# Gates of the last stage in three groups of 12, 9 and 4 tiles, and three tiles more closed by TensorE

## The chip, the cores and the metric

The kernel runs on one core of a Trainium2 chip. A core has engines that run side by side and wait for each other through semaphores: TensorE (PE, matrix products; PEld is its weight load), VectorE (DVE), ScalarE (ACT), GpSimd (POOL) and SyncE (SP), which here only issues DMAs. Each engine takes its instructions in the order in which they stand in its queue. The metric is the device time of one execution in microseconds (us); lower is better.

## The reference

A two-layer graph network over 3125 nodes with 256 features and 50000 edges. Each layer adds to x a graph convolution, an attention over all nodes and a feed-forward part. The change lies in the last of these, the feed-forward part of layer 1, which is a mixture of four experts:

```python
def _forward(x, edge_index, W_gat, att_src, att_dst, b_gat, ln_gamma, ln_beta, W1, b1, W2, b2):
    ...
    agg = segment_sum(msg, dst, num_segments=M).reshape(M, HEADS * NUM_EXPERTS) + b_gat
    scores = _layernorm(agg, ln_gamma, ln_beta).reshape(M, HEADS, NUM_EXPERTS).mean(1)
    topk_s, topk_i = jax.lax.top_k(scores, TOP_K)
    w = jax.nn.softmax(topk_s, axis=-1)
    out = jnp.zeros_like(x)
    for ei in range(NUM_EXPERTS):
        g = jnp.where(topk_i == ei, w, 0.0).sum(-1)
        hh = jax.nn.gelu(x @ W1[ei] + b1[ei], approximate=False)
        out = out + g[..., None] * (hh @ W2[ei] + b2[ei])
    return out
```

`agg` comes from a small graph attention over edges that are sorted by their target node. The result of the whole network is x plus this `out`.

## The kernel before

The nodes lie in 25 tiles of 128 (the last holds 53), node on the partition. For DMAs the tiles form seven chunks, `CHUNKS`: tiles 0-3, 4-7, 8-11, 12-15, 16-18, 19-21 and 22-24, called chunks 0 to 6 here.

The last stage is `layer1_ffn`. All experts' outputs are computed for all nodes first (L1981 to L2022). The outputs of experts 0 and 1 stay in SBUF (`out0`, shown as `acc` in the profile, and `y1`, shown as `y`); those of experts 2 and 3 go to DRAM (`yd`) and are fetched back by chunks (`fetch`, L2227): chunks 0 to 2 into `yback`, chunks 3 to 5 into the memory of `xT`, chunk 6 into the `yback` that chunk 0 leaves. Beside the experts, POOL gathers and VectorE sums the attention's messages along the sorted edges. What is left then is the closing part, where the change is:

- L2291: for each of the 25 tiles POOL gathers the node's sums from DRAM, `g_r`, one gather after the other.
- `gates` (L2296) makes the four gates of the nodes of one group of tiles: some 36 small VectorE instructions over the whole group, and three steps on ACT: an exponential (L2308), a square root (L2329) and another exponential (L888). The root and the exponential behind it each need a table load on ACT. `gates` is a generator: it hands back control after the first exponential, after the root with the sums beside it, and after the ranks; whoever calls `next` decides what is put between.
- `by_rows` (L2362) closes one tile on VectorE: four instructions, each x += gate x expert output (L2366).
- `by_products` (L2370) closes tiles on TensorE: ACT scales the identity by a gate into a diagonal matrix, four for a tile (`diag`, L2381, three buffers); PE adds up x and the four diagonal products in PSUM (L2383, L2385), and ACT copies the sum back into x (L2373). The copy of a tile is put behind the diagonals of the next. It is a generator too, one tile for each `next`.
- `done` (L2352) counts the tiles of a chunk, and sends the chunk's rows of x to the output when the last has been closed (L2358, SP's queue). SP issues in the order in which `done` found the chunks complete in the program.

Four engines are scheduled by hand here: within PE, VectorE, ACT and SP the program's order is the queue's order, so where the `next` calls stand in lines L2392 to L2414 decides what waits behind what. Before the change the nodes have two groups, tiles 0 to 11 and 12 to 24. Products close tiles 0, 1, 2, 4, 5, 6, 8, 9, 10 of the first and 15, 17, 19, 21, 23 of the second; VectorE closes the eleven others by rows.

Of the kernel before, what the change touches and what calls it, by code (L numbers as in the profile page):

```python
# [23 lines left out]
NT = 25  # L24
# [111 lines left out]
class Kernel:  # L136
# [1795 lines left out]
    def layer1_ffn(self, acc=None):  # L1932
# [4 lines left out]
        with ExitStack() as c:  # L1937
# [358 lines left out]
            def gates(t0, n, out):  # L2296

                s = slice(t0, t0 + n)
                heads, each = [P, n, 4, 4], [P, n, 16]
                rs = r[:, s]  # L2300
                hasb = self.has[:, s, None].to_broadcast([P, n, 4])
                d = ga.tile([P, n, 4], F32, name=f"g_d{n}")
                nc.vector.tensor_sub(d, rs[:, :, 20:24], loop[:, s])
                c2 = ga.tile([P, n, 2, 4], F32, name=f"g_c2{n}")
                nc.vector.tensor_scalar(c2[:, :, 0, :], d, 0.0, None, op0=OP.min)
                nc.vector.scalar_tensor_tensor(c2[:, :, 1, :], d, 0.0, hasnt[:, s, None].to_broadcast([P, n, 4]),
                                               op0=OP.max, op1=OP.mult)
                nc.scalar.activation(c2, c2, AF.Exp)  # L2308
                yield
                nc.vector.tensor_mul(c2[:, :, 0, :], c2[:, :, 0, :], hasb)  # L2310
                nc.vector.tensor_mul(d, rs[:, :, 16:20], c2[:, :, 0, :])
                nc.vector.scalar_tensor_tensor(d, d, 1e-16, c2[:, :, 1, :], op0=OP.add, op1=OP.add)
                nc.vector.reciprocal(d, d)
                nc.vector.tensor_mul(c2, c2, d[:, :, None, :].to_broadcast([P, n, 2, 4]))
                agg = ga.tile(each, F32, name=f"agg{n}")
                own = ga.tile(each, F32, name=f"g_own{n}")
                for v, dest, i in ((rs[:, :, 0:16], agg, 0), (srow[:, s, 0:16], own, 1)):
                    nc.vector.tensor_mul(dest.rearrange("p t (h e) -> p t h e", h=4),
                                         v.rearrange("p t (h e) -> p t h e", h=4),
                                         c2[:, :, i, :, None].to_broadcast(heads))  # L2320
                nc.vector.tensor_add(agg, agg, own)
                nc.vector.tensor_add(agg, agg, vec["b_gat"][:, None, :].to_broadcast(each))
                mu = ga.tile([P, n], F32, name=f"s_mu{n}")
                nc.vector.tensor_reduce(mu, agg, AX.X, OP.add)
                nc.vector.scalar_tensor_tensor(agg, mu[:, :, None].to_broadcast(each), -1.0 / 16, agg,
                                               op0=OP.mult, op1=OP.add)
                nc.vector.tensor_mul(own, agg, agg)
                nc.vector.tensor_reduce(mu, own, AX.X, OP.add)
                nc.scalar.activation(mu, mu, AF.Sqrt, bias=self.eps, scale=1.0 / 16)  # L2329
                nc.vector.tensor_mul(agg, agg, vec["ln_gamma"][:, None, :].to_broadcast(each))  # L2330
                sc = ga.tile([P, n, NE], F32, name=f"s_sc{n}")
                nc.vector.tensor_reduce(sc, agg.rearrange("p t (h e) -> p t e h", h=4), AX.X, OP.add)
                yield
                nc.vector.reciprocal(mu, mu)
                nc.vector.tensor_mul(sc, sc, mu[:, :, None].to_broadcast([P, n, NE]))
                nc.vector.tensor_add(sc, sc, beta[:, None, :].to_broadcast([P, n, NE]))
                gate = self.softmax_parts(ga, sc, n, NE, f"s{n}")
                mask = self.top_two(ga, sc, n, NE, f"s{n}", tie)
                yield
                nc.vector.tensor_mul(gate, gate, mask)  # L2340
                self.normalise(ga, gate, n, NE, f"s{n}")
                out.append((gate, t0))
# [4 lines left out]
            def parts_of(t):  # L2347
                t0 = CHUNKS[chunk_of[t]][0]
                p, b = held(t), back[t0]
                return p, [out0[:p, t, :], y1[:p, t, :], b[:p, 0, t - t0, :], b[:p, 1, t - t0, :]]  # L2350

            def done(t):  # L2352
                i = chunk_of[t]
                left[i] -= 1
                if left[i] == 0:
                    t0, n = CHUNKS[i]
                    for s, p in pieces(t0, n):
                        nc.sync.dma_start(token_rows(self.out, t0, s, p), self.x[:p, t0 + s.start:t0 + s.stop, :])  # L2358
                    if i + 2 * HOMES < len(CHUNKS):
                        fetch(*CHUNKS[i + 2 * HOMES])  # L2360

            def by_rows(t, gate, g0):  # L2362

                p, vs = parts_of(t)
                for ei in range(NE):
                    nc.vector.scalar_tensor_tensor(self.x[:p, t, :], vs[ei], gate[:p, t - g0, ei:ei + 1],  # L2366
                                                   self.x[:p, t, :], op0=OP.mult, op1=OP.add)
                done(t)

            def by_products(tiles, gate, g0):  # L2370

                def settle(t, py):
                    nc.scalar.copy(self.x[:, t, :], py)  # L2373
                    done(t)

                summed = None
                for t in tiles:
                    _, vs = parts_of(t)
                    dg = ga.tile([P, NE, 128], F32, name="diag", bufs=3)
                    for ei in range(NE):  # L2380
                        nc.scalar.activation(dg[:, ei, :], self.ident, AF.Copy, scale=gate[:, t - g0, ei:ei + 1])  # L2381
                    py = ps_y.tile([P, D], F32, name="fpy")
                    nc.tensor.matmul(py, self.ident, self.x[:, t, :], start=True, stop=False)  # L2383
                    for ei in range(NE):
                        nc.tensor.matmul(py, dg[:, ei, :], vs[ei], start=False, stop=(ei == NE - 1))  # L2385
                    if summed is not None:
                        settle(*summed)
                    summed = t, py
                    yield
                settle(*summed)  # L2390

            found = []  # L2392
            for _ in gates(0, 12, found):
                pass
            first = by_products((0, 1, 2, 4, 5, 6, 8, 9, 10), *found[0])
            second = gates(12, NT - 12, found)
            for t in (3, 7, 11):
                next(first)
                by_rows(t, *found[0])
            for n in (2, 1, 2):  # L2400
# [4 lines left out]
                pass  # L2405
            for _ in first:
                pass
            first = by_products((15, 17, 19, 21, 23), *found[1])
            for t in (12, 13, 14, 16, 18, 20, 22):
                by_rows(t, *found[1])  # L2410
                next(first, None)
            for _ in first:
                pass
            by_rows(NT - 1, *found[1])  # L2414


    def edge_column(self, pool, ap, dtype, name, width=1):
# [267 lines left out]
```

## Time and profile before

| | |
|---|---|
| median of 3 runs | 2459.14 us (2455.91 to 2460.01) |
| profiled execution: time, span | 2454.27 us, 2452.5 us |
| first instruction of the first group's gates | 2399.23 us |
| first product (PE) | 2410.06 us |
| second group's gates: first instruction, first row closed with them | 2416.86 us, 2427.81 us |
| last row-closed tile ends on VectorE | 2443.54 us |
| last copy out of PSUM on ACT starts | 2444.48 us |
| busy 2410 to 2444.5 (34.5 us): PE, VectorE, ACT, POOL | 33.49, 29.61, 24.05, 3.20 us |

Times in the profile count from the span's start. A timeline line is: start, duration, engine, line of the kernel, operation, output<-inputs, shapes and how often, and in brackets how long the engine had been idle before and who released it. Matmuls are pipelined and their ends modelled, so start-to-start distances say more than durations. An f32 product shows as two records. "Granted clock" is the share of full speed that TensorE was given.

### The profile page before, as it was taken

Reading aid. Unit: us, or ns where it says so; the run is one execution under the profiler, and the core shown is the slowest. Engines: PE = TensorE matmul, PEld = TensorE weight load, DVE = VectorE, ACT = ScalarE, POOL = GpSimd, SP = SyncE. Lnnn points to the kernel's source line nnn. Section 1 sums busy time; section 2 is a strip of 40 time slices with the busy share of each in tenths; the row PEclk is TensorE's granted clock in tenths of the full one; section 3 lists DMA queues with packets and bytes.
Section 4 is the critical chain, followed back from the end, with each engine's and each line's share of the span. In section 5 each row is a group of like instructions: output and inputs, shape, how many; then the busy total and the mean of one; then the engine's idle time right before and its main releaser. Section 6 shows DMA issues by size and latency. Waiting matters only on the chain.

```text
span 2452.5 us, 27755 instructions
## 1 busy us (share of the span) xinstructions
PE 2001.3 (82%) x8319; PEld 1415.0 (58%) x8319; DVE 1472.7 (60%) x3952; ACT 835.4 (34%) x1852; POOL 1562.2 (64%) x1924
## 2 busy tenths in 40 slices
PE   1666699899889989899999547777769779999955
PEld 0444355445555668789999435545546566677634
DVE  6888948986823696122222458898886962233346
ACT  1353144564513112333434323444430142222314
POOL 5888888886000562777777157777776437777742
PEclk9985799899957999999999779999989869999977
DMA  8613538223001125677887432222222112113242
GB/s 270 225 57 111 223 137 273 71 100 108 12 1 35 66 82 171 205 256 245 261 258 239 130 82 55 57 54 56 55 60 47 34 28 38 28 21 81 58 140 68
DMA packets 200603, 275.75 MB, mean 112 GB/s; under 512 B 58562, under 2 KB 159415, under 8 KB 200443
## 3 DMA queue, kind: packets, MB, share of 16 engines
q1 hardware_dynamic: 146815, 224.49, 27.4%
q0 software_dynamic: 48480, 44.59, 8.8%
q10 hardware_dynamic: 5148, 4.80, 0.7%
q8 instruction: 68, 1.11, 0.2%
q14 instruction: 92, 0.75, 0.1%
HBM read 195.35 MB, written 78.42 MB: 112 GB/s over the span
## 4 chain that ended last, share of the span: by engine, by line
PE 59%; DVE 24%; issue 5%; ACT 5%; DMA 5%; POOL 2%; ACTq 0%; DVEq 0%; SPq 0%; POOLq 0%
PE pb L1207 8%; PE pb L599 7%; PE pc L1219 7%; PE fph L1987 7%; PE fpy L2003 7%; DVE v L1748 3%; PE pc L599 3%; PE pw L1754 2%; PE pb L972 2%; PE pc L985 2%; PE pb L281 2%; PE pb L643 2%; DMA g<-tab,t_src 1%; POOL g L76 1%; PE pc L1484 1%
## 5 line engine op out<-in xcount | busy, mean ns | idle before, releaser
L76 POOL DMA_INDIRECT g<-tab,t_src x391 | 377.3, 965 | 198.1 <-issue 151.1
L83 POOL DMA_INDIRECT adj<-ch_sum,ch_place x391 | 416.4, 1065 | 91.9 <-issue 54.3
L83 POOL DMA_INDIRECT sorted<-src,pos x256 | 245.2, 958 | 134.9 <-issue 102.1
L76 POOL DMA_INDIRECT G<-tabg,g_src x256 | 256.9, 1003 | 78.0 <-DMA G<-tabg,g_src 39.3
L1754 PE MATMUL pw<-v,hot 128*128 128x260 f32 x782 | 215.1, 436 | 0.0
L1207 PE MATMUL pb<-xs,w 128*128 128x128 f32 (+1 forms) x1248 | 205.5, 324 | 9.2 <-issue 8.6
L599 PE MATMUL pb<-adj,sup 128*128 128x448 f32 (+1 forms) x484 | 195.6, 549 | 15.1 <-DVE r_tot L1354 13.6
L1207 PEld LDWEIGHTS pb<-xs,w 128*128 128x128 f32 x1248 | 187.7, 194 | 25.8 <-issue 9.6
L1219 PE MATMUL pc<-w,h 128*128 128x256 f32 x896 | 199.7, 379 | 0.0
L1209 ACT ACTIVATE h<-pb,b 128x128 f32<-128x128 f32 (+1 forms) x312 | 129.1, 414 | 176.2 <-PE pb L1207 106.9
L1754 PEld LDWEIGHTS pw<-v,hot 128*128 128x128 f32 x782 | 165.7, 217 | 30.0
L1219 PEld LDWEIGHTS pc<-w,h 128*128 128x128 f32 x896 | 167.3, 190 | 21.2
L2003 PE MATMUL fpy<-fw,fh 128*128 128x256 f32 (+1 forms) x800 | 177.7, 379 | 0.0
L1987 PE MATMUL fph<-xT,fw 128*128 128x512 f32 (+2 forms) x448 | 174.1, 542 | 0.0
L83 POOL DMA_INDIRECT slots<-rows,abi x50 | 58.9, 1178 | 177.8 <-DVE abi L1110 167.9
L2003 PEld LDWEIGHTS fpy<-fw,fh 128*128 128x128 f32 (+1 forms) x800 | 149.6, 187 | 31.8 <-issue 8.5
L1466 ACT ACTIVATE s_z<-s_y,s_val 128x128 f16<-128x128 f16 x256 | 112.4, 486 | 122.6 <-issue 108.2
L1989 ACT ACTIVATE fh<-fph,cols 128x512 f32<-128x512 f32 (+2 forms) x112 | 70.2, 633 | 215.6 <-PE fph L1987 215.6
L599 PEld LDWEIGHTS pb<-adj,sup 128*128 128x128 f32 x484 | 90.0, 193 | 91.8 <-issue 85.5
L1987 PEld LDWEIGHTS fph<-xT,fw 128*128 128x128 f32 x448 | 85.3, 191 | 76.0 <-issue 54.9
L1748 DVE TENSOR_TENSOR v<-msg,own_bank 128x2048 f32<-128x2048 f32 (+2 forms) x50 | 111.9, 2239 | 1.7
L298 POOL MEMSET idle<- 128x128 f32 x441 | 99.2, 225 | 0.3
(591 smaller groups left out, 3674.9 us busy)
## 6 DMA issues: line engine op xcount, KB each, us to landing
adj<-zero SPq DMA_DIRECT2D x25, 1600.0 KB
w<-in_L_ffn_W1p_dram SPq DMA_DIRECT2D x39, 1024.0 KB
w<-in_L_ffn_W2p_dram SPq DMA_DIRECT2D x39, 1024.0 KB
adj<-adj SPq DMA_DIRECT2D x24, 896.0 KB
adj<-adj SPq DMA_DIRECT2D x24, 704.0 KB
slots<-empty SPq DMA_DIRECT2D x1, 7392.0 KB
adj<-ch_sum,ch_place POOLq DMA_INDIRECT x391
g<-tab,t_src POOLq DMA_INDIRECT x391
```

The source lines that it names most:

```text
L76: return nc.gpsimd.indirect_dma_start(out=out, out_offset=None, in_=table, in_offset=bass.IndirectOffsetOnAxis(ap=idx, axis=0))
L83: return nc.gpsimd.indirect_dma_start(out=table, out_offset=bass.IndirectOffsetOnAxis(ap=idx, axis=0), in_=rows, in_offset=None, **kw)
L298: rest = self.nc.gpsimd.memset(self.idle, 0.0)
L599: nc.tensor.matmul(pm[:, :w], sup[:, b, k * 128:(k + 1) * 128], mats[b, h][:, c0 - PARTS[h][0]:c0 - PARTS[h][0] + w], start=(b == b0), sto ...
L1207: nc.tensor.matmul(ph[:, :m], w1[:, k, f * 128:(f + 1) * 128], xs[:, k, :m], start=(k == 0), stop=(k == 1))
L1209: ins = nc.scalar.activation(h[:, f, :m], ph[:, :m], AF.Gelu, bias=b1[:, f:f + 1])
L1219: nc.tensor.matmul(py, h[:, f, i * 128:(i + 1) * 128], w2[:, f, :], start=(f == 0), stop=(f == FC - 1))
L1466: nc.scalar.activation(z[:, i, k, :], y, AF.Relu, bias=val[:, k, s], scale=val[:, 2 + k, s])
L1748: self.latest = nc.vector.tensor_mul(v[:, :n, :, :HD], o[:, :n, None, :HD].to_broadcast([128, n, 4, HD]), weight[:, :n, :, None].to_broadc ...
L1754: nc.tensor.matmul(pw.rearrange("p h c -> p (h c)"), hot[:, k, :], v[:, k, :, :].rearrange("p h c -> p (h c)"), start=(k == 0), stop=(k == ...
L1987: nc.tensor.matmul(ph[:, :m], w1[:, k, f * 128:(f + 1) * 128], xT[:, k, t0 * P:t0 * P + m], start=(k == 0), stop=(k == 1))
L2003: nc.tensor.matmul(py[:p], hs[:, f, i * P:i * P + p], w2[:, f, :], start=(f == 0), stop=(f == FC - 1))
```

## The change

The second group of 13 tiles is split into one of 9 (tiles 12 to 20) and one of 4 (21 to 24). Tile 11 is closed later, between the third group's steps. Products now close 0, 1, 2, 4, 5, 6, 8, 9, 10, then 12, 13, 15, 16, 18, 19, then 21 and 22; VectorE closes 3, 7, 11, 14, 17, 23, 24 and, last of all, 20. Chunk 6 is therefore complete before chunk 5 in the program's order.

```diff
             first = by_products((0, 1, 2, 4, 5, 6, 8, 9, 10), *found[0])
-            second = gates(12, NT - 12, found)
-            for t in (3, 7, 11):
+            second, third = gates(12, 9, found), gates(21, NT - 21, found)
+            for t in (3, 7):
                 next(first)
                 by_rows(t, *found[0])
             for n in (2, 1, 2):
                 next(second)
                 for _ in range(n):
                     next(first)
             for _ in second:
                 pass
             for _ in first:
                 pass
-            first = by_products((15, 17, 19, 21, 23), *found[1])
-            for t in (12, 13, 14, 16, 18, 20, 22):
-                by_rows(t, *found[1])
-                next(first, None)
+            first = by_products((12, 13, 15, 16, 18, 19), *found[1])
+            for t in (11, 14, 17):
+                next(third)
+                next(first)
+                by_rows(t, *found[0 if t < 12 else 1])
+            for _ in third:
+                pass
+            for _ in range(3):
+                next(first)
+            second = by_products((21, 22), *found[2])
+            next(second)
             for _ in first:
                 pass
-            by_rows(NT - 1, *found[1])
+            by_rows(23, *found[2])
+            for _ in second:
+                pass
+            by_rows(NT - 1, *found[2])
+            by_rows(20, *found[1])
```

## The prediction

> **What bounds the kernel now.** I read the page's 40 slices first: the last stage holds only the last two or three, so I then went by the chain of waits, the windows and the timeline from 2396 us on. The chain of waits from 2434 us to the end holds one engine:
>
> ```profile
> 2440.55 1.73 PE fpy L2385 x8
> 2442.28 0.43 PE fpy L2383 x2
> 2442.71 1.74 PE fpy L2385 x8
> 2444.48 0.37 ACT x L2373
> ```
>
> A tile closed by products costs PE 0.43 + 1.73 = 2.16 us, and the tiles follow each other without a gap. The windows (columns: length, busy time of PE, PEld, DVE, ACT, POOL, then granted clock, DMA share, GB/s) say how full PE is:
>
> ```profile
> 2416.00:2422.00 6.00, 6.00 (x29) 5.28 (x29) 4.40 (x15) 3.93 (x13) 0.00 (x0) 1.00 0.26 79
> 2422.00:2428.00 6.00, 5.45 (x26) 4.34 (x25) 5.26 (x20) 5.96 (x15) 0.00 (x0) 1.00 0.34 108
> 2434.00:2440.00 6.00, 6.00 (x29) 5.28 (x29) 5.68 (x13) 4.89 (x17) 0.00 (x0) 1.00 0.64 215
> ```
>
> PE is full at granted clock 1.00 but for two short holes, the first of them in the middle window. The timeline shows what makes them, and where VectorE ends:
>
> ```profile
> 2424.85 1.28 ACT L888 ACT_TABLE_LOAD   x1
> 2426.15 0.25 ACT L888 ACTIVATE sm_exs<-sm_exs 128x52 f32<-128x52 f32 x1
> 2426.30 1.26 ACT L2381 ACTIVATE diag<-ident,sm_exs 128x128 f32<-128x128 f32 x4
> 2426.74 0.70 PE L2385 MATMUL fpy<-acc,diag 128*128 128x256 f32 x2 [0.55 <-ACT diag L2381]
> ...
> 2433.81 0.70 PE L2385 MATMUL fpy<-acc,diag 128*128 128x256 f32 x2 [0.33 <-ACT diag L2381]
> ...
> 2442.55 0.99 DVE L2366 SCALAR_TENSOR_TENSOR x<-yback,sm_exs,x 53x256 f32<-53x256 f32 x2
> ```
>
> Wherever ACT does something for the gates between two tiles' diagonals, PE waits for the diagonal. VectorE ends at 2443.54, PE at 2444.48: the two are about balanced, and PE is the later.
>
> **The change part by part.**
>
> *Three tiles from VectorE to PE.* Products go from 9 + 5 = 14 to 9 + 6 + 2 = 17, rows from 11 to 8. VectorE saves 3 x 1.96 = 5.9 us (a tile by rows starts every 1.96 us: 2409.61, 2411.57, 2413.55). That is off the path. PE gets 3 x 2.16 = **+6.5 us**, and it has no idle time to put them in. PE's start doesn't move: it waits for the gates of tiles 0 to 11, whose work is untouched (first product at 2410.06).
>
> *The second group starts earlier.* It waited for the last gather and had one more row-tile ahead of it:
>
> ```profile
> 2407.91 0.95 POOL L76 DMA_INDIRECT g_r<-sums,g_ati  x1 [0.30 <-issue]
> ...
> 2416.86 0.21 DVE L2303 TENSOR_TENSOR g_d<-g_r,loop 128x52 f32<-128x52 f32 x1 [1.28 <-DMA g_r<-sums,g_ati]
> ```
>
> The first row is tile 20's gather. Tile 11's was usable 2.74 us after its start (2396.49 to 2399.23), tile 24's 3.69 us (2413.17 to 2416.86); so tile 20 is there by 2411.6, and the group starts when the rows of tile 7 end, at 2413.55, 3.3 us earlier. POOL's queue is as before. But the ACT steps of the group stand between product tiles in ACT's queue, and those go at PE's pace: the square root now follows the copy of tile 2 (2419.26), its table load ends at 2420.95, and the exponential runs at 2424.08, after a second load. VectorE, ready with the sums at about 2418.4, waits, and its gates are done at 2425.35 instead of 2427.81. PE still has tiles of the first group until 2433, so the gain reaches nobody. PE's wait at that exponential is about as before (0.96 for 0.81): **+0.1**.
>
> *The third group is new.* On VectorE 36 small instructions, about 7 us at 0.2 us each (rows of 16 elements take 0.17, those of the 12-tile group 0.21 to 0.49). On ACT an exponential, two table loads of 1.28, a root, an exponential. The built order on ACT says where they stand, and I lay them out from the rows:
> - First exponential: behind the copy of tile 10, which waits for PE until 2433.18. VectorE has finished the rows of tile 11 at 2427.9 and waits some 5.8 us; behind it are the rows of 14, 17, 23, 24 and 20, all off the path. The diagonal of tile 12 starts at 2433.65, PE at 2434.10. Before, the hole here made 0.59; now 0.79: **+0.2**.
> - Root: the load runs from 2434.93 to 2436.23. VectorE resumes at 2433.73 and needs the stretch to the sum of squares, 4.13 us for 12 tiles and 4.30 for 13, so 0.17 a tile and 2.77 for 4: the root runs at 2436.75, tile 13's diagonal starts at 2436.96, and PE begins it at 2437.42 (a diagonal's start to PE's: 0.46). Its turn was 2436.36: with 0.1 for the restart **+1.2**.
> - Second load: behind the copy of tile 12, 2438.58 to 2439.86. VectorE goes through the rows of 14 first (to 2439.1) and gives the exponential's input at 2440.2. Tile 15's diagonal starts at 2440.40, PE at 2440.85, where its turn was 2439.68: **+1.3**.
> - From there ACT is ahead again (1.65 us a tile to PE's 2.16). Tile 21's gates are ready at 2444.15 and not wanted until 2447.5.
>
> Bounds of the 2.77: from below 2.4 (12 instructions at 0.2), from above 4.30; I take the line through both groups, and keep +1.5 as the high end. Both stalls may vanish at the low end if ACT stays a tile ahead (0 instead of 2.5).
>
> *The end.* PE ends at 2444.48 + 6.5 + 0.1 + 0.2 + 1.2 + 1.3 = 2453.7. Behind it SP's queue now has chunk 6 (309 KB), which waits for tile 22's copy, and only then chunk 5 (384 KB), though that is ready: tile 20's rows end near 2450. Before, chunk 5 had been sent at 2442.72 and only chunk 6 was left:
>
> ```profile
> 2446.00:2446.50 0.50, 0.00 (x0) 0.00 (x0) 0.00 (x0) 0.00 (x0) 0.00 (x0) 1.00 0.97 332
> 2446.50:2447.00 0.50, 0.00 (x0) 0.00 (x0) 0.00 (x0) 0.00 (x0) 0.00 (x0) 0.59 0.49 119
> ```
>
> 384 KB at 332 GB/s are **+1.2**; between 0 (hidden beside chunk 6) and 1.6 (one issue of 0.37 more).
>
> **Sum:** 9.3 + 1.2 = **+10.5 us**. The profiled execution took 2454.27 (span 2452.5), which would become 2464.8; it lies 4.9 under the median of the runs, 2459.14, which becomes 2469.6.
>
> *A rule on table loads.* The rows show no more than 1.30 us from the load's start to the next activation (2424.85 to 2426.15). [...] I go by the row, since the copy in front ends 0.01 to 0.02 us before the load.
>
> **The rivals.**
> 1. *Only the tiles count.* ACT stays far enough ahead, the two new stalls vanish: 6.5 + 0.3 + 1.2 = +8.0, 2467.1. For it: diag has three buffers. Against it: before, the same pair of loads cost PE 0.81.
> 2. *PE's clock falls in the stalls.* It can, in an earlier stage of this trace:
>
> ```profile
> 1718.52 3.77 PE L1754 MATMUL pw<-v,hot 128*128 128x260 f32 x16
> ...
> 1737.75 0.35 PE L1722 MATMUL psm<-ident,top 4*128 4x4 f32 x2 [2.63 <-DVE top L1717]
> 1738.03 6.43 PE L1754 MATMUL pw<-v,hot 128*128 128x260 f32 x16
> 1744.30 1.05 PE L1852 MATMUL pdots<-kv 128*128 128x128 f32 x8
> ```
>
> After idle times of 1.02 and 2.63 the same 16 matmuls took 6.43 in place of 3.77 (granted clock 0.58 there), while single waits of 1.52 and 1.68 left it at 1.00. Mine are 1.1 and 1.2 with 1.8 us of work between, on the safe side of that, not by much. Price 2.7: +13.2, 2472.3; with the gates at their high end too (+1.5) +14.7, 2473.8.
> 3. *PE wasn't the bound.* If VectorE set the end, the new end is its own: 2425.35, less 2 us of its waits for ACT, + 6 x 1.96 + 7 = 2442.1, 1.4 under the 2443.54 of before: 2457.7 before the later DMA is counted, so not slower. It decides only if 17 products fit into the 34.4 us that 14 took, 2.02 us each; the rows have 2.16 with PE busy 6.00 of 6.00.
> 4. *The floor.* The two holes of before vanish as well: 6.5 - 1.4 = +5.1, 2464.2, with the DMA hidden.
>
> **How the numbers follow.** Forecast 0.50, only the tiles 0.22, clock 0.18, floor 0.06, VectorE 0.04. Faster or slower is told from no change by 0.2%, 4.9 us. The floor lies on that border and goes to "same" with part of the last case: slower 0.90, same 0.07, faster 0.03. The runs before spread from 2455.91 to 2460.01; the range goes from 6.5 above the lowest, 2462, to 15 above the highest, 2475.
>
> **What would show it.** The last copy of PSUM near 2453.7 in a span of about 2463; 17 tiles of 2.16 at clock 1.00; VectorE idle some 5 to 6 us after the rows of tile 11; a PE wait for diag of about 1 us before each of the second and third tile of the second group; the output of tiles 19 to 21 as the last DMA. It is wrong if PE shows no waits there, if the clock dips below 1.00 between 2437 and 2443, or if VectorE's row of tile 20 ends after PE.

## The result, and the profile after

The changed kernel takes 2467.87 us, median of 9 runs (2462.67 to 2474.42); the kernel before took 2457.26 us beside it (2450.72 to 2460.28, 9 runs). The ratio is 1.0045, with an interval of 1.003 to 1.0061: slower by 10.6 us of the medians. The forecast was 2469.6 us and +10.5. The interval, put on 2457 us, is 7.4 to 15.0 us, so that the medians alone would have agreed with other sums too; the test of the sum is the stage itself.

The profiled execution took 2467.87 us (span 2466.2), 13.7 us of span more than before. Not all of that is the change. The stage's first product (the first with a diagonal; tile 0's product of x runs far ahead, at 2379.43) starts at 2413.50 instead of 2410.06, because what stands ahead of it, whose code is the same, ran 3.44 us longer in this execution. I therefore measure the stage by itself, in two stretches:

| | before | changed | difference | forecast |
|---|---|---|---|---|
| A: first product to the start of the last copy out of PSUM | 34.42 us | 43.19 us | +8.77 | +9.3 |
| tail: start of the last copy to the span's end | 8.02 us | 9.51 us | +1.49 | +1.2 |
| C = A + tail | 42.44 us | 52.70 us | +10.26 | +10.5 |
| first product to the end of VectorE's last row | 33.48 us | 39.65 us | +6.17 | +6.4 |

The chain of waits of the changed kernel, its end (start, duration, what), answers to the four chain lines of before:

```profile
2436.39 0.37 ACT x L2373
2436.93 0.19 DVE g_c L2310
...
2439.75 0.22 DVE s_mu L2328
2440.14 0.26 DVE s_sc L2332
...
2441.87 0.48 DVE x L2366
...
2443.10 0.19 DVE sm_exs L887
2443.30 0.22 ACT sm_exs L888
2443.52 0.30 ACT diag L2381
2443.86 1.99 PE fpy L2385 x8
...
2454.92 1.74 PE fpy L2385 x8
2456.69 0.37 ACT x L2373
```

Before, this chain held PE alone from 2434 us to the last copy. Now it leaves PE at 2436.39, runs through the third group's gates on VectorE and ACT, with the rows of tile 14 (L2366) in the middle of them, and comes back to PE at 2443.86. From there on it is PE again, tile after tile. The windows of the changed kernel (length, busy time of PE, PEld, DVE, ACT, POOL, then granted clock, DMA share, GB/s) show the same two parts:

```profile
2436.00:2446.00 10.00, 7.77 (x34) 5.90 (x33) 8.18 (x34) 8.64 (x24) 0.00 (x0) 1.00 0.16 54
2446.00:2456.50 10.50, 10.50 (x50) 9.03 (x48) 6.69 (x17) 6.57 (x22) 0.00 (x0) 1.00 0.27 91
```

PE idles for 2.23 us of the ten in which the third group's gates are worked out, and is full afterwards. The granted clock is 1.00 in both. The timeline of PE says which waits those 2.23 us are:

```profile
2437.24 0.70 PE L2385 MATMUL fpy<-acc,diag 128*128 128x256 f32 x2 [0.45 <-ACT diag L2381]
2440.65 0.70 PE L2385 MATMUL fpy<-acc,diag 128*128 128x256 f32 x2 [0.99 <-ACT diag L2381]
2443.86 0.70 PE L2385 MATMUL fpy<-acc,diag 128*128 128x256 f32 x2 [0.79 <-ACT diag L2381]
```

These are tiles 12, 13 and 15, each waiting for its diagonal. ACT's timeline of the changed kernel shows what stands in front of those diagonals:

```profile
2436.66 0.23 ACT L2308 ACTIVATE g_c<-g_c 128x32 f32<-128x32 f32 x1
2436.79 1.26 ACT L2381 ACTIVATE diag<-ident,sm_exs 128x128 f32<-128x128 f32 x4
2438.07 1.28 ACT L2329 ACT_TABLE_LOAD   x1
2440.01 0.30 ACT L2329 ACTIVATE s_mu<-s_mu,eps 128x4 f32<-128x4 f32 x1 [0.65 <-DVE s_mu L2328]
2440.21 1.26 ACT L2381 ACTIVATE diag<-ident,sm_exs 128x128 f32<-128x128 f32 x4
2441.38 0.35 ACT L2373 COPY x<-fpy 128x256 f32<-128x256 f32 x1
2441.75 1.28 ACT L888 ACT_TABLE_LOAD   x1
2443.30 0.22 ACT L888 ACTIVATE sm_exs<-sm_exs 128x16 f32<-128x16 f32 x1 [0.28 <-DVE sm_exs L887]
2443.43 1.26 ACT L2381 ACTIVATE diag<-ident,sm_exs 128x128 f32<-128x128 f32 x4
```

The exponential stands before the diagonal of tile 12, a table load and the root before that of 13, a second load and the second exponential before that of 15. Twice ACT also waits for VectorE, 0.65 and 0.28 us. On VectorE the changed kernel shows the wait that was forecast for the third group and, at the end, the row of tile 20:

```profile
2417.03 0.19 DVE L2303 TENSOR_TENSOR g_d<-g_r,loop 128x36 f32<-128x36 f32 x1
2424.61 0.21 DVE L2334 RECIPROCAL s_mu<-s_mu 128x9 f32<-128x9 f32 x1 [2.12 <-ACT s_mu L2329]
...
2436.93 0.17 DVE L2310 TENSOR_TENSOR g_c<-g_c,g_has 128x16 f32<-128x16 f32 x1 [6.05 <-ACT g_c L2308]
...
2452.14 1.01 DVE L2366 SCALAR_TENSOR_TENSOR x<-xT,sm_exs,x 128x256 f32<-128x256 f32 x2
```

The second group starts 3.53 us after the first product (6.80 before). VectorE ends at 2453.15, 3.5 us ahead of PE. Behind the last copy SP sends chunk 6 and then tiles 19 to 21, seen in four windows of the changed kernel:

```profile
2458.00:2458.50 0.50, 0.00 (x0) 0.00 (x0) 0.00 (x0) 0.00 (x0) 0.00 (x0) 1.00 0.97 332
2458.50:2459.00 0.50, 0.00 (x0) 0.00 (x0) 0.00 (x0) 0.00 (x0) 0.00 (x0) 1.00 0.95 250
2459.00:2459.50 0.50, 0.00 (x0) 0.00 (x0) 0.00 (x0) 0.00 (x0) 0.00 (x0) 1.00 0.72 219
2459.50:2460.00 0.50, 0.00 (x0) 0.00 (x0) 0.00 (x0) 0.00 (x0) 0.00 (x0) 1.00 0.88 252
```

### The profile page after: what moved, and what is told of

The parts are those of the page before. It is cut to its first block, busy times and chain, and to the rows that moved or that the text cites. A ratio compares the mean times of both kernels' runs of the same rounds, so it can differ in the third digit from the quotient of the medians.

```text
span 2466.2 us, 27858 instructions
## 1 busy us (share of the span) xinstructions
PE 2007.7 (81%) x8349; PEld 1419.7 (58%) x8349; DVE 1470.7 (60%) x3973; ACT 842.3 (34%) x1872; POOL 1563.3 (63%) x1924
## 4 chain that ended last, share of the span: by engine, by line
PE 57%; DVE 18%; POOL 10%; issue 5%; DMA 5%; ACT 3%; DVEq 0%; SPq 0%; ACTq 0%; POOLq 0%
PE pb L1207 8%; PE pc L1219 7%; PE pb L599 7%; PE fph L1987 7%; PE fpy L2003 7%; POOL adj L83 7%; DVE v L1748 3%; PE pb L972 3%; PE pc L599 3%; PE pc L985 3%; PE pw L1754 2%; PE pb L643 2%; DMA g<-tab,t_src 2%; POOL g L76 1%; POOL idle L298 1%
## 5 line engine op out<-in xcount | busy, mean ns | idle before, releaser
L599 PE MATMUL pb<-adj,sup 128*128 128x448 f32 (+1 forms) x484 | 196.8, 552 | 14.4 <-DVE r_tot L1354 13.7
```

Source lines behind the costliest of these rows:

```text
L599: nc.tensor.matmul(pm[:, :w], sup[:, b, k * 128:(k + 1) * 128], mats[b, h][:, c0 - PARTS[h][0]:c0 - PARTS[h][0] + w], start=(b == b0), sto ...
```

## The experiments

The theory under test is the forecast's sum: three more tiles on PE, two stalls where ACT works on the third group's gates, and a longer output at the end. Against it stand "only the tiles count" and "VectorE sets the end". The first four kernels ran on another chip, whose earlier stages are longer: the kernel before takes 2832.24 us there (median of 31 runs, 2812.47 to 2854.09). A few us can hardly be told from its times, so the verdicts on those rest on A, the tail and C, measured in one profiled execution of each; a tile closed by products takes 2.16 us there too. The other four ran with the kernel before at 2455.46 us (23 runs, 2451.51 to 2460.95). The ratios are given as measured, with their 95% intervals; they are not the quotients of these medians. One thing moves A and C without any edit: the first two tiles by products took between 5.47 and 7.00 us in the eight kernels that don't warm PE (6.85 before, 6.73 changed; see the last section).

### The tiles alone

The two groups of before, but eight products and five rows in the second:

```diff
-            first = by_products((15, 17, 19, 21, 23), *found[1])
-            for t in (12, 13, 14, 16, 18, 20, 22):
+            first = by_products((13, 15, 16, 18, 19, 21, 22, 23), *found[1])
+            for t in (12, 14, 17, 20):
                 by_rows(t, *found[1])
-                next(first, None)
+                next(first)
```

> Edit to the kernel before: its two groups of 12 and 13 tiles stay; only the split of the tiles changes to that of the changed kernel, 17 by products and 8 by rows (second group: products 13, 15, 16, 18, 19, 21, 22, 23; rows 12, 14, 17, 20, 24). The chunks are completed in order. Measured by two stretches that don't depend on the earlier stages: A, from PE's first diag product to the start of the last copy out of PSUM (before 34.42 us, changed 43.19), and C, from that product to the end of the span (before 42.44, changed 52.70). Theory 1 (PE's queue sets the end): three tiles of 2.16 us: A 40.9, C 48.9, total +6.5 us, ratio about 1.0026, and VectorE's last row ends 5 to 6 us earlier than before in the stage. Rival (VectorE sets the end): A and C shrink, C about 38, a gain of 4 us. Rival (the third group alone costs the time, the tiles are hidden): A 34.4, C 42.4, no change.

It took 2840.98 us, ratio 1.0012 (0.9983 to 1.0041). A was 40.65 us, the tail 7.91, C 48.56: 6.1 more than before, with first two tiles that were 0.47 faster (6.38 us). Free of those is the stretch from the second group's first product to the last copy: 18.06 us for eight tiles, where it was 11.59 for five, so 6.47 more. PE ran the eight tiles at 2.16 us each after the one old hole. Here the end of VectorE's last row, and the last copy on ACT:

```profile
2832.46 0.48 DVE L2366 SCALAR_TENSOR_TENSOR x<-y,sm_exs,x 53x256 f32<-53x256 f32 x1
2832.97 0.99 DVE L2366 SCALAR_TENSOR_TENSOR x<-yback,sm_exs,x 53x256 f32<-53x256 f32 x2
```

```profile
2846.89 0.37 ACT L2373 COPY x<-fpy 128x256 f32<-128x256 f32 x1 [1.79 <-PE fpy L2385]
```

VectorE ends 27.72 us after the first product, 5.8 us earlier than before, and that freed nothing: the last copy comes 13 us behind it. So three tiles moved to PE cost their full price, and this is the part of the change that is 6 of its 10 us. The rest, about 4 us, belongs to the third group and to the order at the end.

### The groups alone

Three groups of 12, 9 and 4, with the fourteen products of before:

```diff
-            second = gates(12, NT - 12, found)
-            for t in (3, 7, 11):
+            second, third = gates(12, 9, found), gates(21, NT - 21, found)
+            for t in (3, 7):
...
+            first = by_products((15, 17, 19), *found[1])
+            for t in (11, 12, 13):
+                next(third)
+                next(first)
+                by_rows(t, *found[0 if t < 12 else 1])
+            for _ in third:
+                pass
+            second = by_products((21, 23), *found[2])
+            next(second)
             for _ in first:
                 pass
+            for t in (14, 16, 18, 20):
+                by_rows(t, *found[1])
+            for _ in second:
+                pass
+            by_rows(22, *found[2])
+            by_rows(NT - 1, *found[2])
```

> Edit to the kernel before: its three groups become 12, 9 and 4 as in the changed kernel, with the third group's steps put where the changed kernel has them, but the tiles closed by products stay the 14 of before (15, 17, 19 in the second group, 21 and 23 in the third) and VectorE closes 11. Chunks are completed in order, chunk 6 last. Theory 1: PE alone would end at A = 36.9 (34.4 and the stalls of 2.3 us at the third group's root and second exponential); but VectorE now waits about 6 us for the third group's first exponential, does its 36 instructions (about 7 us) and still has six rows of 1.96 us behind them: its last row ends about 45 us after the first product (before 33.5), and C is about 53, +10 us, so the group costs VectorE more than three rows save it. Rival (only the number of product tiles counts; the group is hidden): C 42.4, no change. Rival (only the two stalls count): C 44.9, +2.5 us.

It took 2850.05 us, ratio 1.0035 (0.9998 to 1.0072); C was 52.62 us, as long as the changed kernel's 52.70, with three products fewer. But another engine sets it. A is only 39.13 (2.2 above the 36.9 expected, most of it, 1.7 us, at tile 21, whose diagonal waited for the third group's last steps behind rows on VectorE); VectorE ends 46.11 us after the first product and the span 6.51 us after that. Two lines of VectorE's timeline carry it, the wait for the third group's exponential and the last row (the span is 2834.6 us):

```profile
2806.11 0.18 DVE L2310 TENSOR_TENSOR g_c<-g_c,g_has 128x16 f32<-128x16 f32 x1 [6.05 <-ACT g_c L2308]
...
2827.10 0.99 DVE L2366 SCALAR_TENSOR_TENSOR x<-yback,sm_exs,x 53x256 f32<-53x256 f32 x2
```

So the third group costs VectorE about 12.6 us (46.11 against 33.48): its own instructions and 6.05 us of waiting for ACT, in which the rows behind it stand still. Three groups do not pay for VectorE unless rows are taken off it, and the three tiles that are taken off it cost PE what the first experiment showed.

### The output in the order of readiness

The changed kernel, with the row of tile 20 ahead of the last products, so that chunk 5 goes out before SP waits for tile 22:

```diff
             by_rows(23, *found[2])
+            by_rows(20, *found[1])
             for _ in second:
                 pass
             by_rows(NT - 1, *found[2])
-            by_rows(20, *found[1])
```

> Edit to the changed kernel: the rows of tile 20 are put before those of tile 24, and before the last products are drained, so that chunk 5 (384 KB) is sent before chunk 6 as in the kernel before. Theory 1: the last DMA is then chunk 6 alone; the stretch from the last copy to the end of the span falls from 9.51 to about 8.0 (before 8.02), C from 52.70 to 51.2; A stays 43.2. Rival (chunk 5's transfer is hidden beside chunk 6): no change, 9.5.

The tail was 7.86 us instead of 9.51, as expected: the term of the end is this order. It took 2849.79 us, ratio 1.0044 (1.0014 to 1.0075). Of SP's queue only two pieces are left after the last copy (at 2851.04 of a span of 2858.9), where the changed kernel has three; the first line below is this kernel's, from SP's timeline, the second the changed kernel's:

```profile
2851.44 0.74 SPq L2358 DMA_DIRECT2D out_dram<-x  x2
```

```profile
2457.09 1.21 SPq L2358 DMA_DIRECT2D out_dram<-x  x3
```

The third issue is 0.47 of the 1.65 us; that the transfer of the 384 KB makes the rest is argued, from the four windows above. A was 41.92 us instead of 43.19, and this was not expected: the first two tiles took 3.31 and 2.16 us instead of 3.57 and 3.16, with the same instructions in front of them. C, 49.78, is for that reason 1.4 below the expected 51.2. The stretch of the second and third groups was as in the changed kernel, 20.49 us from the second group's first product to the last copy against 20.50.

### The third group's ACT steps ahead of PE's turn

The changed kernel, with the third group's exponential, root and second exponential beside the first group's last products, where ACT has tiles in hand:

```diff
             for _ in second:
                 pass
+            next(third)
+            next(first)
+            next(third)
+            next(first)
+            next(third)
+            later = by_products((12, 13, 15, 16, 18, 19), *found[1])
+            next(later)
             for _ in first:
                 pass
-            first = by_products((12, 13, 15, 16, 18, 19), *found[1])
-            for t in (11, 14, 17):
-                next(third)
-                next(first)
-                by_rows(t, *found[0 if t < 12 else 1])
             for _ in third:
                 pass
-            for _ in range(3):
-                next(first)
+            for t in (11, 14, 17):
+                by_rows(t, *found[0 if t < 12 else 1])
+                next(later)
+            for _ in range(2):
+                next(later)
...
-            for _ in first:
+            for _ in later:
                 pass
```

> Edit to the changed kernel: the third group's steps are taken right after the second group's, beside the products of tiles 9 and 10, and the products of the second group begin before the last copy of the first; the rows of tile 11 come after. Groups, tiles by products and the order of the last rows stay. Theory 1: the stalls of PE for diag at tiles 12, 13 and 15 (2.88, 3.41 and 3.22 us between tiles in place of 2.16, together 3.0 us too long) leave one of about 0.9 at tile 12's, behind the second table load; A falls from 43.19 to about 41.1, C from 52.70 to 50.6, the kernel stays some 8 us slower than before. Rival (table loads cost PE the same wherever they stand): A stays about 43.

It took 2843.62 us, ratio 1.0031 (0.9991 to 1.007). The stretch from the second group's first product to the last copy fell from 20.50 to 18.25 us; with the same eight products and two groups it had been 18.06 in the first experiment. From 2812 us to the last copy PE's timeline of this kernel has two waits for a diagonal left:

```profile
2814.72 0.70 PE L2385 MATMUL fpy<-acc,diag 128*128 128x256 f32 x2 [0.55 <-ACT diag L2381]
2824.18 0.70 PE L2385 MATMUL fpy<-acc,diag 128*128 128x256 f32 x2 [0.53 <-ACT diag L2381]
```

The first is still in the first group's stretch, the second at tile 12; those at tiles 13 and 15 are gone. So the two stalls (together 2.3 us, of which the stretch lost 2.25) are a matter of where the ACT steps stand in its queue, and not of what they cost. "Only the tiles count" would have had them vanish in the changed kernel itself. A was 41.90 where 41.1 was expected: the 0.8 lie in the first tiles (3.57, 3.43 and 2.69 us), which this edit does not touch. Of these, 0.27 are the second tile, at half clock for longer (6.1 us from the first product, 5.6 in the changed kernel; estimates, see the last section), and 0.53 the third, whose diagonal stands behind the second group's first exponential: VectorE gave its input late, after waits of 1.59, 0.91 and 0.83 us among the rows of tile 7 and the group's first steps, whose cause the profile doesn't show.

### Both mends in one

> Edit to the changed kernel: both mends together, the third group's steps early and the rows of tile 20 before those of tile 24, so that of the change only the split of tiles and the groups' sizes are left. Measured also by B, from PE's first product of x in the second group to the last copy (before 11.59 for 5 tiles, changed 20.50 for 8), and the tail from the last copy to the end of the span (before 8.02, changed 9.51). Theory 1: B 18.3, tail 7.9, C about 48.9, still 6.4 us above the kernel before, which is the three tiles. Rival (the group and its table loads were the cost): C about 43.

The edit is the last two diffs together. It took 2459.66 us (one run), with A at 40.84, the tail at 7.99 and C at 48.83 us, 0.1 from the expected 48.9. That is 3.87 below the changed kernel, and the two mends alone gave 2.25 and 1.65. What is left above the kernel before, 6.39 us, is the three tiles (3 x 2.16 us; the first two tiles were 0.27 faster than before, tile 12's hole 0.20 longer). No order of the same work that I found makes the three-group kernel the faster one. That giving tiles back to VectorE would not either is an estimate, not a run: VectorE ends 35.91 us after the first product here, with eight rows; three rows more, at 1.96 us, make 41.8, and with some 6.5 us behind the last row C would be 48.3.

### One tile back to VectorE

If the kernel before is bound by PE alone, a tile moved the other way gains; if the two engines are balanced, it costs. In the kernel before, tile 23 goes from products to rows:

```diff
-            first = by_products((15, 17, 19, 21, 23), *found[1])
-            for t in (12, 13, 14, 16, 18, 20, 22):
+            first = by_products((15, 17, 19, 21), *found[1])
+            for t in (12, 13, 14, 16, 18, 20, 22, 23):
```

> Edit to the kernel before in the opposite direction of the change: tile 23 by rows in place of by products, 13 products and 12 rows. Theory 1: PE ends 2.16 us earlier (A 32.3), but VectorE's last row comes 1.96 later, 35.4 after the first product, and the last output with it: C about 43.2 to 43.5, some 0.9 us more than before, so that the kernel before was already within a tile of its balance. Rival (PE alone sets the end, VectorE has room): C 40.3.

It took 2458.53 us (one run, which tells nothing of 1 us), and C was 41.25: 1.2 below before, where 0.9 above was expected. This expectation failed. A (31.31) and the end of VectorE (34.85 us after the first product) were not far from it (32.3 and 35.4), and what is missing isn't the edit's doing: the first two tiles took 5.69 us instead of 6.85, and VectorE had the last gather 0.3 us sooner after the first product and didn't wait for the root. One row of 1.96 us on top of the 33.48 of before makes 35.4, and with 6.4 behind it C would be some 0.6 below before, not 1.2. What I had wrong is what follows VectorE's last row. The span is 2456.8, and VectorE's last row and SP's last issue in this kernel are

```profile
2449.41 0.99 DVE L2366 SCALAR_TENSOR_TENSOR x<-yback,sm_exs,x 53x256 f32<-53x256 f32 x2
```

```profile
2450.42 0.26 SPq L2358 DMA_DIRECT2D out_dram<-x  x1
```

The row ends at 2450.40 and the span 6.40 us later, since only the last piece of 53 KB is still to go. In the second experiment it was 6.51. From the end of PE's last copy it takes 7.5 to 7.65 us where that copy sets the end (tails of 7.86 to 8.02 us less the copy's 0.37). I put the difference down to the piece of 256 KB that tile 23 holds back besides; in the kernel before, SP sends these two after the copy.

```profile
2444.88 0.74 SPq L2358 DMA_DIRECT2D out_dram<-x  x2
```

So in the kernel before VectorE, at 33.48 us, would have allowed an end at 33.48 + 6.45 = 39.9 us (6.45 lies between the two); the stage took 42.44. VectorE had 2.5 us to spare, not the 0.94 by which its last row precedes PE's last copy.

### A warm clock

PE comes to its first product after 32.63 us without one in the kernel before, and the first tiles run at a granted clock of 0.50 (2410.00 to 2413.60 us) and then 0.66 (to 2416.90). Ten products that nobody reads, on PE while the first group's gates are still worked out, are added to the kernel before; they take the gates as weights and a resident tile as moving data:

```diff
                 nc.vector.tensor_mul(c2, c2, d[:, :, None, :].to_broadcast([P, n, 2, 4]))
+                if t0 == 0:
+                    for _ in range(10):
+                        ph = ps_h.tile([128, 4 * P], F32, name="fph")
+                        nc.tensor.matmul(ph[:8 * n, :D], c2.rearrange("p t a h -> p (t a h)"), out0[:, 0, :],
+                                         start=True, stop=True)
...
-            for n in (2, 1, 2):
+            for n in (3, 1, 1):
```

> Edit to the kernel before: ten products that nothing reads (weights: the gates' exponentials of the first group, moving operand: tile 0 of the first expert's output) run on PE while the first group's gates are still being made, so that PE's clock is up when the first tile comes; and the second group's root is put one product tile later in ACT's queue (3, 1, 1 tiles in place of 2, 1, 2 between its steps). Groups, tiles and rows stay. Theory 1 (PE's queue sets the end, at half clock for its first 6 us): the first two tiles take 2.2 us each in place of 3.6 and 3.3 to 2.3, A falls from 34.42 by 2 to 3 us to about 31.7, and then VectorE's last row, 33.5 after the first product, is what the last output waits for: C falls from 42.44 only to about 41.3. Rival (the ramp costs nothing, ACT's diagonals set the pace there): A stays 34.4. Rival (VectorE sets the end): C stays 42.4. The whole gain, 1.1 us, is under what the timed ratio can tell.

The first tiles came at 1.84 and 2.15 us instead of 3.58 and 3.27, and the granted clock is 1.00 from 2417 to 2421 us, where they begin at 2417.34. The stage doesn't start later for it: from the first instruction of the gates to the first product it is 10.83 us, as before. C was 40.36 us, 2.1 below before and 0.9 below what was expected. The execution of before had slow first tiles, though; against the 5.47 to 7.00 us that the first two took in all kernels without warming, their 3.99 us are a gain of 1.5 to 3.0 us on PE, and not always 2.9. VectorE ends 33.86 us after the first product and the span 6.50 us behind it. One stall of 1.1 us is new: the second group's first exponential now stands before a diagonal that PE wants sooner, and waits for VectorE, which itself waits for the last gather:

```profile
2424.28 0.29 ACT L2308 ACTIVATE g_c<-g_c 128x104 f32<-128x104 f32 x1 [2.37 <-DVE g_c L2306]
```

The time was 2453.5 us, ratio 0.999 (0.9978 to 1.0002): a gain of 2 us by the stage in one execution, which the times do not prove.

The second form keeps the warming products and adds one more tile for VectorE in the first group (rows 3, 7, 11, 10), six products in the second, and the second group's first diagonal ahead of the first group's last copy:

```diff
-            first = by_products((0, 1, 2, 4, 5, 6, 8, 9, 10), *found[0])
+            first = by_products((0, 1, 2, 4, 5, 6, 8, 9), *found[0])
...
-            for t in (3, 7, 11):
+            for t in (3, 7, 11, 10):
...
+            later = by_products((15, 17, 19, 21, 22, 23), *found[1])
+            next(later)
             for _ in first:
                 pass
-            first = by_products((15, 17, 19, 21, 23), *found[1])
-            for t in (12, 13, 14, 16, 18, 20, 22):
+            for t in (12, 13, 14, 16, 18, 20):
...
```

> Edit to the kernel before, two groups of 12 and 13: the warming products of the previous run, and the two engines' shares moved to fit: tile 10 by rows in the time that VectorE waited for the last gather, tile 22 by products in its place (products 0, 1, 2, 4, 5, 6, 8, 9, then 15, 17, 19, 21, 22, 23), and the second group's first diagonal before the first group's last copy. Theory 1: PE's last copy at A 31.8, VectorE's last row at about 32.2, C about 40.0, 2.4 us less than the kernel before; ratio about 0.999. Rival (nothing is left to gain in the stage because the last gather sets it): C 42.

C was 39.61 us, 2.8 below before, and the two engines now end 0.2 us apart (31.62 and 31.85). Its median, 2452.63 us, is 2.8 below the kernel before's; the ratio is 0.9994 (0.9983 to 1.0004), so that by the times alone it is not told from it. By the stage it is well below the changed kernel (C of 52.70).

## Why the prediction was right

The total, +10.5, came out at +10.26 in the stage and +10.6 in the medians. That the medians came within 0.1 is luck, given their interval of 7.4 to 15.0. The term by term reading:

| step | forecast | measured | by |
|---|---|---|---|
| three tiles on PE | +6.5 | +6.47 (the added tiles at 2.15 to 2.16); done alone +6.1 in C, +6.47 from the second group's first product on | trace, first experiment |
| hole at tile 12 | +0.2 | +0.13 (2.88 us to the next tile, 2.75 before) | trace |
| stall at tile 13, root | +1.2 | +1.25 (3.41 for 2.16) | trace |
| stall at tile 15, second load | +1.3 | +1.06 (3.22 for 2.16) | trace |
| exponential of the second group | +0.1 | 0.0 (2.97 us, 2.98 before) | trace |
| clock | 0 | -0.12 (first two tiles 6.73 us, 6.85 before) | trace |
| output order | +1.2 | +1.49; 1.65 taken away by the order alone | trace, third experiment |

Two misses of some 0.25 us, at tile 15 and at the end, have opposite signs, and part of the closeness of the sum is owed to that. The clock's nothing is owed to luck as well: the first two tiles happened to run alike in the two executions, while runs with the same code up to there differ by up to 1.5 us.

*The stalls.* Both came where the built order on ACT had put them, and for the reason given: an in-order queue, in which a gate's step delays the diagonals behind it (PE waited 0.99 and 0.79 us for them). The general sentence in front of it, that PE waits wherever ACT does something for the gates, was too broad. In the kernel before two of the second group's steps stand between diagonals and cost PE 0.00 and 0.05 us, because ACT was ahead there:

```profile
2417.47 0.29 ACT L2308 ACTIVATE g_c<-g_c 128x104 f32<-128x104 f32 x1
2421.81 1.28 ACT L2329 ACT_TABLE_LOAD   x1
```

And the hole at 2433.81 has no step of the gates in front of it: tile 15's diagonal stands behind the first group's last copy, and in the second warm form, which puts it ahead of that copy, tile 15 takes 2.16 us instead of 2.75. The third group took VectorE 33 instructions and 6.75 us, for the 36 and 7 of the forecast. Its stretch to the sum of squares, for which no row existed, was put at 2.77 us by a line through the groups of 12 and 13; it took 2.82 (2436.93 to 2439.75 in the chain, the start of L2310 to the start of L2328). The second stall was sized 0.24 too high. The step at fault is the exponential's input "at 2440.2" and the diagonal at 2440.40, that is 2.78 us after PE had begun tile 13 and 0.20 behind the exponential. In the run it was 2.65 us (2440.65 to 2443.30) and 0.13. The fourth experiment showed that these stalls go when the steps stand elsewhere, which the forecast had only laid out.

*The end.* The mechanism was right, the size 0.3 too low. 384 KB were taken at the 332 GB/s of one window of before, and the windows of the changed kernel show 332, 250, 219 and 252; besides, SP has a third issue to make. How the 0.3 is shared between the two is not shown. The upper bound of 1.6 held.

*The second group and VectorE.* Its start 3.3 us earlier and the wait of 5.8 for the third group's exponential (6.05) are there, and the earlier gates reached nobody, as forecast. The wait for the root was 2.12 us; rival 3 takes 2, but the layout, with the sums at 2418.4 and the load's end at 2420.95, implied some 2.8, because it had the sums 0.6 us too early. The end of tile 20's rows was forecast 39.9 us after the first product and came at 39.65.

*The rivals.* "Only the tiles count" fell with the two stalls. "The clock falls" fell with 1.00 in both windows: waits of 0.99 and 0.79 us with a tile between them left it untouched. "VectorE sets the end" fell with the first experiment. "The floor" fell because the holes of before remained and two came on top.

*What was off without costing the forecast.* The step "the two are about balanced" compared the engines' last instructions. VectorE's slack was 2.5 us and not 0.94, since the span ends 6.4 to 6.5 us behind its last row and 7.5 to 7.65 behind PE's last copy. Rival 3, which left the same tail behind both engines, shares this error.

*The table loads.* The second group's load on ACT, in the changed kernel's timeline, shows 1.30 us from its start to the next activation:

```profile
2426.01 1.28 ACT L888 ACT_TABLE_LOAD   x1
2427.31 0.23 ACT L888 ACTIVATE sm_exs<-sm_exs 128x36 f32<-128x36 f32 x1
```

The copy in front of it ends 0.01 us before the load. The forecast took its loads from such rows of the kernel before, and the stage came out at +10.26 us for the forecast +10.5.

## What to carry to other kernels

In the stage that ends last, a tile moved onto the engine that sets the end costs its full length, however much the other engine gains (here 6.47 us for three tiles of 2.16, while VectorE ended 5.8 us earlier); and balance is read at the end of the outputs behind each engine, not at the engines' last instructions (here 6.4 to 6.5 us behind VectorE's last row, 7.5 to 7.65 behind PE's last copy). Splitting a group of small operations pays for its fixed instructions again (here 33 on VectorE, 6.75 us), and in an in-order queue its steps run at the pace of the tiles they stand between (VectorE waited 6.05 us for the third group's exponential): put them where that queue has tiles in hand, which was worth 2.25 us here. In a queue of outputs put what is ready ahead of what waits, which was worth 1.65.

## What the runs showed of the hardware

The granted clock after a long idle time of PE does not come back at the same moment in runs whose code is the same up to there. In the changed kernel, after 32.85 us of idle time, the first tiles took 3.57 and 3.16 us:

```profile
2413.50:2417.00 3.50, 3.50 (x8) 2.85 (x9) 3.29 (x8) 2.00 (x7) 2.78 (x3) 0.50 0.20 10
2417.00:2420.00 3.00, 3.00 (x10) 2.45 (x9) 2.42 (x12) 1.70 (x6) 0.00 (x0) 0.65 0.16 7
```

and with the order of the output changed, far behind (and on the other chip), after 32.69 us, 3.31 and 2.16:

```profile
2809.10:2812.40 3.30, 3.28 (x8) 2.71 (x9) 3.09 (x8) 2.01 (x7) 2.39 (x4) 0.54 0.19 12
2812.40:2814.60 2.20, 2.20 (x12) 1.92 (x12) 1.70 (x9) 1.81 (x6) 0.77 (x1) 1.00 0.18 9
```

That is 1.3 us on the path with no change in the work, more than several of the terms above. It isn't the chip: on that other one alone the first two tiles took 6.38, 6.80, 5.47 and 7.00 us in the first four experiments. The half speed lasted 3.0 us in the second of these kernels and 6.1 in the fourth experiment. Both are estimates: the first from the granted clock, 0.54 over 3.30 us and then 1.00; the second from PE's timeline, in which two records of a product follow in 0.85 or 0.86 us, as at a clock of 0.50 in the kernel before, until 2805.55, that is 6.1 us after the first product at 2799.42, and in 0.43 from then on. In the kernel before the clock needed about 5.8 us from the first product (the granted clock is 0.66 from 2413.60 to 2416.90, which is half speed for 2.2 of these 3.3 us), in the changed kernel 5.6 (0.50 up to 2419.0, 0.92 in the half microsecond behind it). Warming PE ahead of the stage took the delay away, 2.9 us at the first two tiles against that execution of the kernel before.
